# Deeper buffers in the second graph attention, and a two-part, one-step-later block ending in both attentions

## The chip, the cores and the metric

The kernel runs on one core of one Trainium2 chip. The metric is the device time of one launch in microseconds (us). A step of the work is written for five engines: TensorE (PE), VectorE (DVE), ScalarE (ACT), GpSimd (POOL) and SyncE (SP, which here only issues DMAs). Each engine takes its instructions strictly in the order in which they were recorded, and semaphores order the engines against each other.

## What is computed

Four layers run one after the other on 6250 nodes with 256 features each. Two of them are graph attentions over edges that are sorted by their destination; the change is in these two alone. Cut to what matters:

```python
x = x + gat0(layernorm(x), src, dst)          # first attention: 206250 edges, 4 heads of 64
x = x + routed_ffn(layernorm(x))              # 8 experts, top 2
x = x + weighted_sum(layernorm(x), src, dst, edge_weight)
x = x + gated_ffn(layernorm(x), edge_index)   # its gate is the second attention:
                                              # 131072 edges on 8192 node numbers, 4 heads of 4
# an attention, for every edge (s -> d) and head:
e     = leaky_relu(a_src[s] + a_dst[d])
p     = exp(e - segment_max(e, d)[d])
out_d = sum_over_edges(p * h[s]) / (sum_over_edges(p) + 1e-16)
```

In the last layer the 16 numbers of each node that come out of the second attention go through a layer norm, a mean over heads and a top 2 of 4, and the resulting gates weigh four dense expert outputs that were computed before.

## The kernel before, in words

**Tiles, pieces, blocks.** The sorted edges are cut into tiles of 128 edges, and Q = 8 tiles make a piece. The first attention has 1612 tiles (pieces 0 to 201), the second 787 (pieces 0 to 98, the last with 3 tiles). The nodes are cut into 49 blocks of 128 (0 to 48). For each tile, POOL gathers the rows of the 128 source nodes out of a table in device memory with one indirect DMA (`gathers`, L1299 to L1305).

**The loop.** `gat_stream` (from L1225) runs both attentions. It is a software pipeline written out by hand under `manual_schedule`: the order of instructions on each engine is the order of the Python calls. In step s_ it issues, in this order: the gathers of piece s_; on SP, every fourth step, the load of a batch of edge destinations (`load`, tiles db and kf); `beside()`, which hands in one item of other work; the functions that an earlier step left for this one (list `later`, L1463); for the first attention, `done` for blocks whose sums are whole (`ready`, L1466); `scores` of piece s_ - 2 (L1330 to L1343, DVE: it reads the gathered rows); `turned_hots` of piece s_ + 1 (tile ot); the first part of `sums` for piece q = s_ - 10 (PE: a matmul of each tile's one-hot matrix by its messages); `node_parts` of piece s_; `move_sums` (first attention only); `one_hots` of piece q + 1 (tile oh, L1184); the second part of `sums`; every fourth step the transposes and the two scans that find the greatest score, and `weights` (ACT's Exp, L1374 and L1378, and a DVE product, L1379); at the end of the step the block endings of the second attention, and `messages` of piece q + 1 (L1386 to L1393, DVE). So a piece's messages are made 9 steps, and its sums 10 steps, after its gathers were issued.

**Ending a block.** In the second attention the sums of a block lie in PSUM (tile acc, two buffers). When a block's last tile has been summed, its number goes into `ended`, and `done` (L1836) is called at the end of that step: DVE adds the three parts of the sums (tile a24, L1838), ACT takes an Exp (po, L1840), and DVE divides and combines (L1842 to L1855). On the last block of a group of four, `group` follows at once: the layer norm, the top 2 and the gates (`route`, from L767, 33 small DVE instructions with two turns through ACT), and four `put`s of four DVE instructions each (L1872) are left for `beside()`, with a DMA of the results after the fourth (L1882). `done` also issues on SP the load of that block's dense results, tile yb (L1831).

In the first attention windows of 16 tiles (two pieces) are summed, copied to SBUF by ACT (tile kept, L1422), and moved into the sums of the blocks that they touch by further matmuls (`move_sums`, tile bacc, two PSUM buffers, L1435). When a block is whole, `done` (L1969) runs at the start of the next step: ACT's Exp (po, L1972), seven DVE instructions (L1974 to L1985), the store of the block, and a spread (L1992 to L1996). `normed` (L2001 to L2002 and another spread), `twice` (PE transposes, ACT copy xT, L2012 to L2014) and `logits` follow in the next three steps. After block 43, and after the last, the selection of experts (`chosen`) goes on in later steps, a few DVE instructions a step (L268 to L309).

**Other work in the steps.** `beside()` of the first attention prepares expert parameters; that of the second finishes the dense experts (until about 5478 us) and then does the `put`s.

**Buffers.** A tile name in a pool has a fixed number of buffers, and an instruction that writes a buffer again waits for the last reader of what lay in it. Before the change the second attention has 14 buffers for gathered rows (g; the first has 13), 6 for turned one-hots (ot), 4 for one-hots (oh) and 3 for split messages (s3).

Of the kernel before, what the change touches and what calls it, by code (L numbers as in the profile page):

```python
# [20 lines left out]
F32 = mybir.dt.float32  # L21
BF = mybir.dt.bfloat16
I32 = mybir.dt.int32
I16 = mybir.dt.int16
AF = mybir.ActivationFunctionType
# [7 lines left out]
P = 128  # L33
# [38 lines left out]
def tile_kernel(ctx, tc, src_ins, out):  # L72
    nc = tc.nc
    x_in = src_ins["x"]
    N, D = x_in.shape
# [633 lines left out]
    H0, C0 = I["L0_gnn_att_src"].shape  # L709
    H1, C1 = I["L1_ffn_att_src"].shape  # L710
    D1 = H1 * C1
# [280 lines left out]
    Q = 8  # L992
# [230 lines left out]
    def gat_stream(s, H, CD, si, il, dl, tab, NI, early, done, parts=1, beside=None, pe=None):  # L1223
# [8 lines left out]
        W = DH + 2 * H  # L1232
# [6 lines left out]
        with ExitStack() as st:  # L1239
# [4 lines left out]
            nbw, sums_of, ready, moved = {}, {}, [], []  # L1244
# [10 lines left out]
            mp = pool("gw", 2)  # L1255
# [42 lines left out]

            def gathers(q):  # L1299
                t0, n = span(q)  # L1300
                g = piece[q] = mp.tile([P, Q, W], F32, name="g", bufs=13 if parts == 1 else 14)
                for j in range(n):
                    nc.gpsimd.indirect_dma_start(  # L1303
                        out=g[:, j, :DH + H], out_offset=None, in_=tab,
                        in_offset=bass.IndirectOffsetOnAxis(ap=si[:, t0 + j:t0 + j + 1], axis=0))  # L1305

            def turned_hots(q):
                t0, n = span(q)
                db = dbs.pop(q)
                turned[q] = []  # L1310
                for b, a, m in s.windows(t0, n):
                    o = mp.tile([P, Q * P], BF, name="ot", bufs=4 if s.group else 6)
                    nc.vector.tensor_scalar(o[:, :m * P], db[:, (a - t0) * P:(a - t0 + m) * P], nid[:, b:b + 1], None,  # L1313
                                            op0=OP.is_equal)
                    turned[q].append((b, a, m, o))
# [66 lines left out]
            def messages(q):  # L1382
                t0, n = span(q)
                i, o = divmod(t0, B)
                gh = piece[q][:, :n, :DH].rearrange("p n (h c) -> p n h c", h=H)
                nc.vector.tensor_mul(gh, gh, ps[0][:, o:o + n, :, None].to_broadcast([P, n, H, CD]))  # L1386
                g = piece.pop(q)
                if parts > 1:
                    s3 = split[q] = mp.tile([P, Q, parts, W], BF, name="s3", bufs=3)
                    for k in range(parts):  # L1390
                        nc.vector.tensor_copy(s3[:, :n, k], g[:, :n])  # L1391
                        if k + 1 < parts:
                            nc.vector.tensor_sub(g[:, :n], g[:, :n], s3[:, :n, k])  # L1393
                else:
                    split[q] = g
# [45 lines left out]
            with tc.manual_schedule():  # L1441
                if s.group:
                    load_nodes()
                load(0)
                for q in range(min(3, npiece)):
                    turned_hots(q)
                for q in range(min(2, npiece)):
                    node_parts(q)
                zts, dMs, pzs = {}, {}, {}
                last, s_, later = max(npiece + LAG, PB * nbatch + 7) + 1, -1, []  # L1450

                def follow(a):
                    if a is not None:
                        later.append(a)

                while s_ < last or later or moved or ready:
                    s_ += 1
                    if s_ < npiece:
                        gathers(s_)
                    if PB <= s_ + 3 < npiece:  # L1460
                        load(s_ + 3)
                    beside()
                    now, later[:] = list(later), []  # L1463
                    for f, a in now:
                        follow(f(*a))
                    while ready:  # L1466
                        b = ready.pop(0)
                        follow(done(b, sums_of.pop(b), items.pop(b), mp))
                    k, q = s_ - 2, s_ - LAG
                    if 0 <= k < npiece:  # L1470
                        scores(k)
                    i = k // PB - 1
                    at = k % PB if 0 <= i < nbatch else None
                    if 3 <= k + 3 < npiece and k >= 0:
                        turned_hots(k + 3)
                    beside()
                    if 0 <= q < npiece:
                        sums(q, 0)
                    if at == 2:
                        pzs[i] = turn_back(*dMs.pop(i))  # L1480
                    if 0 <= k and k + 2 < npiece:
                        node_parts(k + 2)
                    move_sums()
                    if at == 1:
                        dMs[i] = greatest(i, zts.pop(i))
                    if 0 <= q + 1 < npiece:
                        hots[q + 1] = one_hots(s, q + 1, mp, ips, dl, 3 if s.group else 4, F32 if parts == 1 else BF)
                    beside()
                    if 0 <= q < npiece:
                        sums(q, 1)  # L1490
                    if at == 0:
                        zts[i] = turn_scores(i)
                    if at == 3:
                        weights(i, pzs.pop(i))
                    beside()
                    if s.group:
                        keep_sums()
                    while ended:
                        b = ended.pop(0)
                        follow(done(b, acc.pop(b), items.pop(b), mp))  # L1500
                    if 0 <= q + 1 < npiece:
                        messages(q + 1)
                    beside()
                while beside():
                    pass
# [298 lines left out]
    def layer1_fast(s1, si, dl1, il1, HN, tab_1, y_d, rest):  # L1804
# [4 lines left out]
        with tc.tile_pool(name="g1f", bufs=1) as g1, tc.tile_pool(name="f1w", bufs=2) as fp:  # L1809
# [18 lines left out]
            def load_y(b):  # L1828
                if b < NT:
                    ys[b] = fp.tile([P, E1 + 1, D], F32, name="yb", bufs=GB + 1)  # L1830
                    nc.sync.dma_start(ys[b], y_d[b])  # L1831
# [2 lines left out]
                return HN[:, b, :D1]  # L1834

            def done(b, acc, hs_, mp):  # L1836
                a = mp.tile([P, D1 + 2 * H1], F32, name="a24")
                nc.vector.tensor_reduce(a, acc.rearrange("p s w -> p w s"), AX.X, OP.add)  # L1838
                po = mp.tile([P, H1], F32, name="po")
                nc.scalar.activation(po, a[:, W1:], AF.Exp, scale=-1.0)  # L1840
                rd = mp.tile([P, H1], F32, name="rd")
                nc.vector.scalar_tensor_tensor(rd, a[:, D1:W1], 1e-16, po, op0=OP.add, op1=OP.add)  # L1842
                nc.vector.reciprocal(rd, rd)

                def hd(x):
                    return x.rearrange("p (h c) -> p h c", h=H1)

                load_y(b)
                g = b // GB
                if g not in ag:  # L1850
                    ag[g] = fp.tile([P, GB, D1], F32, name="ag")
                o = mp.tile([P, D1], F32, name="o")
                nc.vector.tensor_mul(hd(o), hd(hs_), po[:, :, None].to_broadcast([P, H1, C1]))
                nc.vector.tensor_add(o, o, a[:, :D1])
                nc.vector.tensor_mul(hd(ag[g][:, b % GB, :]), hd(o), rd[:, :, None].to_broadcast([P, H1, C1]))  # L1855
                if b == blocks_in(g)[-1]:
                    group(g)
# [37 lines left out]
    def fast(flag_s0, last_d, dl_d):  # L1895
# [12 lines left out]
        with tc.tile_pool(name="gat0f", bufs=1) as g0:  # L1908
# [58 lines left out]
                return hs  # L1967

            def done(b, acc, hx, mp):  # L1969
                acc, hs, x = acc[:, 0], hx[:, 0], hx[:, 1]  # L1970
                po = mp.tile([P, H0], F32, name="po")
                nc.scalar.activation(po, acc[:, D + H0:], AF.Exp, scale=-1.0)  # L1972
                rd = mp.tile([P, H0], F32, name="rd")
                nc.vector.scalar_tensor_tensor(rd, acc[:, D:D + H0], 1e-16, po, op0=OP.add, op1=OP.add)  # L1974
                nc.vector.reciprocal(rd, rd)
                o = mp.tile([P, D], F32, name="o")

                def hd(a):
                    return a.rearrange("p (h c) -> p h c", h=H0)

                nc.vector.tensor_mul(hd(o), hd(hs), po[:, :, None].to_broadcast([P, H0, C0]))
                nc.vector.tensor_add(o, o, acc[:, :D])
                nc.vector.tensor_mul(hd(o), hd(o), rd[:, :, None].to_broadcast([P, H0, C0]))
                nc.vector.tensor_add(o, o, bias)
                nc.vector.scalar_tensor_tensor(x, o, 0.0, x, op0=OP.max, op1=OP.add)  # L1985
                nc.sync.dma_start(x_d[b * P:(b + 1) * P], x)
                return normed, (b, mp, x) + spread(mp, x)
# [319 lines left out]
```

## Time and profile before

| | us |
|---|---|
| median of the 7 runs shown (6468.51 to 6478.05) | 6474.33 |
| the profiled execution: its time / its span | 6476.74 / 6474.9 |
| first attention, POOL's gathers (first to last start) | 189.7 to 2233.9 |
| second attention, POOL's gathers (first to last start) | 5385.6 to 6390.8 |
| second attention, DVE busy from 5700 to 6300 | 458.9 of 600 |

The profile comes from one execution. A group's row gives the line, the engine, the operation, its output and inputs, how many there were, their busy time and mean duration in ns, and the idle time of the engine just before them with what ended that idle time ("issue": nothing that the profile shows). A timeline's row gives the start, the duration and the same names; a square bracket at its end holds the idle time before it and what ended it. Rows with xN are several like instructions, merged.

### The profile page before, as it was taken

The page shows a single profiled execution, that of the slowest core. Times are in us where ns is not written, and L with a number is a line of the kernel's source. Part 1 is how long each engine was busy: PE and PEld are TensorE (multiplying, and loading weights), DVE is VectorE, ACT ScalarE, POOL GpSimd, SP SyncE. Part 2 cuts the span into 40 slices and gives each one's busy share as a digit, 9 for nine tenths or more (in the row PEclk, how much of TensorE's full clock was granted, in tenths as well). Part 3 has the DMA queues.
Part 4 walks back from the last instruction along what each step waited for, and adds up shares of the span by engine and source line. Part 5 has one row for each costly group of instructions (what it writes and reads, how often), then busy time and mean ns, then how long its engine had stood idle before and what let it go on. Part 6 is the DMA issues. An engine that isn't in the chain of part 4 may idle for free.

```text
span 6474.9 us, 61956 instructions
## 1 busy us (share of the span) xinstructions
PE 3812.3 (59%) x17583; PEld 2863.5 (44%) x17583; DVE 4331.8 (67%) x10445; ACT 1204.3 (19%) x2770; POOL 4094.1 (63%) x4304
## 2 busy tenths in 40 slices
PE   4256666665666679999513777776777677111111
PEld 3144444444444558888402444444444445111111
DVE  5266666666666683444368888888888872777777
ACT  2011111112221112323100222222222222000000
POOL 0677777777777612232147777777777765777773
PEclk9677777778777789999756888887888888555555
DMA  4644445444444335557563444444444442222221
GB/s 131 143 146 144 147 146 148 146 147 146 147 146 144 110 105 196 185 185 235 186 205 113 128 126 129 128 129 125 128 128 127 127 118 84 54 76 76 76 76 56
DMA packets 495995, 856.25 MB, mean 132 GB/s; under 512 B 140310, under 2 KB 345303, under 8 KB 486134
## 3 DMA queue, kind: packets, MB, share of 16 engines
q0 software_dynamic: 190112, 461.21, 26.0%
q1 hardware_dynamic: 280226, 366.94, 17.1%
q10 hardware_dynamic: 25300, 24.00, 1.1%
q8 instruction: 143, 2.34, 0.1%
q14 instruction: 214, 1.75, 0.1%
HBM read 758.44 MB, written 95.50 MB: 132 GB/s over the span
## 4 chain that ended last, share of the span: by engine, by line
POOL 34%; DVE 18%; issue 17%; PE 15%; DMA 14%; ACT 1%; DVEq 0%; SPq 0%; ACTq 0%; POOLq 0%; another core or an unknown queue 0%
POOL g L234 17%; POOL g L1303 17%; DMA g<-tab,si 7%; PE py L647 5%; PE ph L634 4%; DVE g L1386 3%; DMA g<-tab_ef,si 2%; DVE run L2102 2%; PE acc L1409 2%; DMA g<-tab_1f,si1s 2%; DVE oh L1184 2%; DMA xc<-x_d 1%; DVE ot L1313 1%; PE pf L1772 1%; PE pf L1784 1%
## 5 line engine op out<-in xcount | busy, mean ns | idle before, releaser
L234 POOL DMA_INDIRECT g<-tab_ef,si x1616 | 1531.4, 948 | 620.9 <-issue 599.9
L1303 POOL DMA_INDIRECT g<-tab,si x1612 | 1554.3, 964 | 504.3 <-issue 414.3
L2102 DVE SCALAR_TENSOR_TENSOR run<-g,wab,run 128x256 f32<-128x256 f32 x2626 | 1264.2, 488 | 330.5 <-DMA g<-tab_ef,si 252.7
L1409 PE MATMUL acc<-g,oh 128*128 128x264 f32 x3224 | 1000.6, 464 | 307.9 <-DVE g L1386 238.8
L1409 PEld LDWEIGHTS acc<-g,oh 128*128 128x128 f32 x3224 | 719.2, 232 | 484.0 <-DVE g L1386 265.7
L1303 POOL DMA_INDIRECT g<-tab_1f,si1s x787 | 766.7, 974 | 250.1 <-issue 212.4
L2219 PE MATMUL acc<-run,oh 128*128 128x256 f32 x808 | 304.1, 514 | 690.9 <-DVE oh L2106 533.0
L1335 DVE TENSOR_TENSOR z<-g,nd 128x32 f32<-128x32 f32 (+1 forms) x301 | 58.0, 193 | 830.6 <-DMA g<-tab,si 687.3
L1409 PE MATMUL acc<-s,oh 128*128 128x72 bf16 x1267 | 106.4, 249 | 751.9 <-DVE s L1391 751.9
L2219 PEld LDWEIGHTS acc<-run,oh 128*128 128x128 f32 x808 | 191.4, 252 | 794.7 <-issue 462.9
L1772 PE MATMUL pf<-xt,w 128*128 128x512 f32 (+1 forms) x832 | 411.4, 628 | 101.0 <-ACT h L1777 100.9
L1386 DVE TENSOR_TENSOR g<-g,mix 128x2048 f32<-128x2048 f32 x202 | 458.9, 2272 | 0.0
L1409 PEld LDWEIGHTS <-oh 128*128 128x128 bf16 x1267 | 85.8, 127 | 763.7 <-issue 481.0
L1784 PE MATMUL pf<-w,h 128*128 128x256 f32 x1568 | 402.2, 401 | 0.0
L634 PE MATMUL ph<-xe,w 128*128 128x256 f32 x1664 | 377.0, 383 | 3.8 <-DVE xe L622 3.8
L647 PE MATMUL py<-w,h 128*128 128x256 f32 x1664 | 370.1, 380 | 0.0
L610 POOL DMA_INDIRECT xg<-tab_x,gi x104 | 118.3, 1137 | 350.2 <-PE pt L619 276.7
L634 PEld LDWEIGHTS ph<-xe,w 128*128 128x128 f32 x1664 | 317.5, 193 | 46.4 <-DVE xe L622 4.6
L1784 PEld LDWEIGHTS pf<-w,h 128*128 128x128 f32 x1568 | 289.3, 194 | 99.4 <-issue 67.1
L647 PEld LDWEIGHTS py<-w,h 128*128 128x128 f32 x1664 | 313.1, 191 | 39.4
L650 POOL DMA_INDIRECT tab_y<-y,so x104 | 111.9, 1076 | 268.4 <-DVE y L649 263.9
L1772 PEld LDWEIGHTS pf<-xt,w 128*128 128x128 f32 x832 | 164.4, 211 | 250.3 <-issue 124.4
(510 smaller groups left out, 6092.1 us busy)
## 6 DMA issues: line engine op xcount, KB each, us to landing
w<-in_L_ffn_W SPq DMA_DIRECT2D x104, 1024.0 KB
db<-s_d SPq DMA_DIRECT2D x74, 1024.0 KB
yb<-y_d SPq DMA_DIRECT2D x49, 640.0 KB
g<-tab_ef,si POOLq DMA_INDIRECT x1616
g<-tab,si POOLq DMA_INDIRECT x1612
y_d<-y SPq DMA_DIRECT2D x196, 128.0 KB
g<-tab_1f,si1s POOLq DMA_INDIRECT x787
yy<-tab_y SPq DMA_DIRECT2D x7, 1792.0 KB
```

Of the source, the lines that this page charges most:

```text
L234: nc.gpsimd.indirect_dma_start(out=dst, out_offset=None, in_=table, in_offset=bass.IndirectOffsetOnAxis(ap=si[:, t:t + 1], axis=0))
L610: nc.gpsimd.indirect_dma_start(out=xg[:, i, :], out_offset=None, in_=tab_x, in_offset=bass.IndirectOffsetOnAxis(ap=gi[:, 2 * j + i:2 * j + ...
L634: nc.tensor.matmul(ph, w1[:, k, f * P:(f + 1) * P], xe[:, k, :], start=(k == 0), stop=(k == KD - 1))
L647: nc.tensor.matmul(py, hs[f][:, i * P:(i + 1) * P], w2[:, f, :], start=(f == 0), stop=(f == FC - 1))
L1184: nc.vector.tensor_tensor(o[:, :m], ips[:, None, k * P:(k + 1) * P].to_broadcast([P, m, P]), dl[:, a:a + m, None].to_broadcast([P, m, P]), ...
L1303: nc.gpsimd.indirect_dma_start(out=g[:, j, :DH + H], out_offset=None, in_=tab, in_offset=bass.IndirectOffsetOnAxis(ap=si[:, t0 + j:t0 + j ...
L1386: nc.vector.tensor_mul(gh, gh, ps[0][:, o:o + n, :, None].to_broadcast([P, n, H, CD]))
L1409: nc.tensor.matmul(acc[b].rearrange("p s w -> p (s w)"), oh[:, t - a], m_, start=(t == lo), stop=(t == hi))
L1772: nc.tensor.matmul(ph[:, :n], w1[:, e, k, f * P:(f + 1) * P], xts[g][:, k, :n], start=(k == 0), stop=(k == KD - 1))
L1784: nc.tensor.matmul(py[:, :D], hs[g, e, f][:, j * P:(j + 1) * P], w2[:, e, f, :], start=False, stop=(f == FC - 1))
L2102: nc.vector.scalar_tensor_tensor(at[:, i] if j < Q - 1 else r[i], g[:, j, :], w, at[:, i], op0=OP.mult, op1=OP.add)
L2219: nc.tensor.matmul(acc[i], oh[:, k], r[k], start=(q % 2 == 0 and k == 0), stop=(last and k == 1))
```

## The change

The second attention gets 20 buffers for g, 9 for ot, 8 for oh and 4 for s3; those of the first attention stay. The block endings of the second attention are called at the start of the step after the one in which the block ended, in place of the end of that same step. In both attentions `done` is cut in two: it issues the Exp (in the second attention also the addition of the three parts and the load of yb), and returns a function `ending`, which the loop calls a step later and which holds the rest. In the second attention a24 and po get 4 buffers.

```diff
-                g = piece[q] = mp.tile([P, Q, W], F32, name="g", bufs=13 if parts == 1 else 14)
+                g = piece[q] = mp.tile([P, Q, W], F32, name="g", bufs=13 if parts == 1 else 20)
...
-                    o = mp.tile([P, Q * P], BF, name="ot", bufs=4 if s.group else 6)
+                    o = mp.tile([P, Q * P], BF, name="ot", bufs=4 if s.group else 9)
...
-                    s3 = split[q] = mp.tile([P, Q, parts, W], BF, name="s3", bufs=3)
+                    s3 = split[q] = mp.tile([P, Q, parts, W], BF, name="s3", bufs=4)
...
-                while s_ < last or later or moved or ready:
+                while s_ < last or later or moved or ready or ended:
...
                     while ready:
                         b = ready.pop(0)
                         follow(done(b, sums_of.pop(b), items.pop(b), mp))
+                    while ended:
+                        b = ended.pop(0)
+                        follow(done(b, acc.pop(b), items.pop(b), mp))
...
-                        hots[q + 1] = one_hots(s, q + 1, mp, ips, dl, 3 if s.group else 4, F32 if parts == 1 else BF)
+                        hots[q + 1] = one_hots(s, q + 1, mp, ips, dl, 3 if s.group else 8, F32 if parts == 1 else BF)
...
                     if s.group:
                         keep_sums()
-                    while ended:
-                        b = ended.pop(0)
-                        follow(done(b, acc.pop(b), items.pop(b), mp))
                     if 0 <= q + 1 < npiece:
                         messages(q + 1)
...
@@ in layer1_fast, the second attention @@
             def done(b, acc, hs_, mp):
-                a = mp.tile([P, D1 + 2 * H1], F32, name="a24")
+                a = mp.tile([P, D1 + 2 * H1], F32, name="a24", bufs=4)
                 nc.vector.tensor_reduce(a, acc.rearrange("p s w -> p w s"), AX.X, OP.add)
-                po = mp.tile([P, H1], F32, name="po")
+                po = mp.tile([P, H1], F32, name="po", bufs=4)
                 nc.scalar.activation(po, a[:, W1:], AF.Exp, scale=-1.0)
+                load_y(b)
+                return ending, (b, a, po, hs_, mp)
+
+            def ending(b, a, po, hs_, mp):
                 rd = mp.tile([P, H1], F32, name="rd")
...
-                load_y(b)
                 g = b // GB
...
@@ in fast, the first attention @@
             def done(b, acc, hx, mp):
-                acc, hs, x = acc[:, 0], hx[:, 0], hx[:, 1]
                 po = mp.tile([P, H0], F32, name="po")
-                nc.scalar.activation(po, acc[:, D + H0:], AF.Exp, scale=-1.0)
+                nc.scalar.activation(po, acc[:, 0, D + H0:], AF.Exp, scale=-1.0)
+                return ending, (b, acc[:, 0], hx[:, 0], hx[:, 1], po, mp)
+
+            def ending(b, acc, hs, x, po, mp):
                 rd = mp.tile([P, H0], F32, name="rd")
```

## The prediction

> **What bounds the kernel now.** I read the page's costliest groups first, then POOL's waits in each attention, then the timelines of the two tails, since everything that the change touches lies in the two attentions. The groups give POOL's part:
>
> ```profile
> L1303 POOL DMA_INDIRECT g<-tab,si x1612 | 1554.3, 964 | 504.3 <-issue 414.3
> L1303 POOL DMA_INDIRECT g<-tab_1f,si1s x787 | 766.7, 974 | 250.1 <-issue 212.4
> ```
>
> Busy and idle time of the second row together are 1016.8 us; without the 10.6 us ahead of the first gather that is 1006.2 us, and first to last gather starts span 5385.6 to 6390.8. So POOL does nothing but gathers there, each 0.974 us and about 0.305 us of gap. Are those gaps waits? POOL's waits between 5386 and 6392 us (line, releaser, total, times, longest):
>
> ```profile
> POOL g L1303 <- issue: 212.4, 697, 0.3
> POOL g L1303 <- DMA vec<-in_L_ffn_ln_gamma: 10.6, 1, 10.6
> POOL g L1303 <- DMA g<-tab_1f,si1s: 9.4, 31, 0.3
> POOL g L1303 <- DVE ot L1313: 7.9, 26, 0.3
> ```
>
> No wait but the first is longer than 0.3 us, the gap that a gather has with no releaser at all. A gather has never waited for a free buffer. The first attention shows the same (13.4 us ahead of its first gather, no other above 0.3), and its DVE waits 687.3 us for gathered rows at L1335. **In both attentions POOL's own pace is the bound, and what the other engines do shows only after the last gather.** Those two tails are the DVE's. The second, in the DVE's timeline:
>
> ```profile
> 6375.87 0.35 DVE L1333 TENSOR_REDUCE nd<-pd 128x64 f32<-128x192 f32 x1
> 6379.99 0.19 DVE L1335 TENSOR_TENSOR z<-g,nd 128x32 f32<-128x32 f32 x1 [3.77 <-DMA g<-tab_1f,si1s]
> ...
> 6382.42 0.22 DVE L1838 TENSOR_REDUCE a<-acc 128x24 f32<-128x72 f32 x1
> 6382.97 0.16 DVE L1842 SCALAR_TENSOR_TENSOR rd<-a,po 128x4 f32<-128x4 f32 x1 [0.33 <-ACT po L1840]
> ...
> 6390.67 0.29 DVE L1386 TENSOR_TENSOR g<-g,pe 128x128 f32<-128x128 f32 x1
> ...
> 6396.84 0.19 DVE L1335 TENSOR_TENSOR z<-g,nd 128x32 f32<-128x32 f32 x1
> ```
>
> At 6379.99 the DVE waits for rows for the last time (piece 96, step 98). Then it ends block 43 and runs the gates of its group (6382.42 to 6390.67), and when it reaches the scores of piece 97 at 6396.84 the rows are there. From there it is dense to 6469.64, where the last output DMA issues.
>
> **The change, part by part.**
>
> *Buffers.* Nothing waits for g on POOL, and in the second attention the DVE's largest waits for anything but gathered rows are for ACT (18.8 us at L1379, 16.1 us at L1842). 0 us, by the rows above; the pace hides the rest. If a wait for a buffer sat in the gaps, it would be at most 0.305 - 0.300 us on 786 gathers, 4 us.
>
> *Moved instructions in the steady part.* In the second attention a block's a24, po and yb load pass messages and, on SP, sometimes the next db and kf loads; the ending is a step later; in the first attention seven DVE instructions and the chain behind them (normed, xT, logits, the tab_x store on SP) are a step later. SP already issues out, yb, db, kf and two more yb in one bunch (5750.35 to 5754) a batch ahead of their use, and a step is about 10 us, so nothing comes late. All this is hidden by POOL's pace: 0 us.
>
> *Tail of the second attention, a hole.* Block 43 ends in step 98. Now a24 runs at the start of step 99, ahead of the scores of piece 97, but the ending and the gates only at the start of step 100, behind them. So the DVE is through with step 98 at 6382.42 + 1.96 (messages, 6390.67 to 6392.63) = 6384.38, does a24 and nd (0.22 + 0.35) and waits for piece 97 from about 6384.96. The last gather of piece 96 starts at 6377.09 and its rows are used at 6379.99, 2.90 us later; the last gather of piece 97 starts at 6387.07, so its rows come at 6389.97. **The DVE stands for 5.0 us, in which it now does gates,** and that work has to be done afterwards. With the sooner landing that the chain of waits has for the gather of 5547.91, 2.28 us, the hole is 4.4; with the longest DMA that the chain of waits shows for gathered rows here, 6.05 us, it is 8.2; with none at all (the DVE busy with something else) it is 0.
>
> *Tail of the second attention, stalls that go.* The 0.33 us between a24 and rd goes for blocks 43 to 47 (5 x 0.33 = 1.65): a step lies between. For block 48 it stays, as nothing else is left. The 0.43 us in which a24 of block 48 waits for PE at 6459.94 goes: the gates of 44 to 47 now come after the last messages and cover that matmul. The yb load of block 48 is nearer to its use: 7.63 us from a24 (6459.94) to the first product (6467.57), less 0.48 us that SP takes; the DMA of it and of out is done at 6463, 4.5 us after issue, so it still fits. Sum of this tail: 5.0 - 1.65 - 0.43 = **+2.9 us.**
>
> *Tail of the first attention.* The last gather starts at 2233.89, the DVE's last wait for rows is 2.35 us at 2232.16. Shifted from before that wait to after it: the logits of block 44 and one step's share of the select (2228.06 to 2229.46), +1.4. Then ACT, where L1379 waits for it:
>
> ```profile
> 2253.70 0.37 ACT L2014 COPY xT<-mix 128x256 f32<-128x256 f32 x1 [5.17 <-PE mix L2012]
> 2254.09 1.28 ACT L1374 ACT_TABLE_LOAD   x1
> 2255.38 0.26 ACT L1374 ACTIVATE mix<-zt 128x128 f32<-128x128 f32 x1
> 2255.55 0.19 ACT L1378 ACTIVATE g<-zt 128x32 f32<-128x32 f32 x1
> ```
>
> The xT copy, queued ahead of the Exp in the same step, waits for a long row of matmuls; the DVE stands 2.30 us, and 0.94 us in the same place at 2282.46. A step later for xT parts the two. In its place normed's sd stands ahead of the Exp: sd 0.33, from the load to L1379 1.69 (2254.09 to 2255.78), less the one-hot (1.13) that the DVE does meanwhile, leaves 0.9 us each time. 2.30 + 0.94 - 1.8 = 1.4 gained. At the end, po of block 48 (2295.45) now stands behind both sd of block 47 and a table load; following the new order with the old durations I get 47's Exp at about 2289.1, its ending (3.2), sd, normed and sd (0.35 + 1.45 + 0.35), load 1.28, and po at 2296.0, +0.5. Sum: 1.4 - 1.4 + 0.5 = **+0.5 us**; from -3 (every such ACT stall gone, the shift hidden) to +4 (neither gain, the end 2 us worse).
>
> *Two rules of the Trainium skill.* The built order has 46 fewer ACT table loads, 1.28 us each in the rows with the Exp 0.01 us behind: 59 us of ACT time, hidden but for what is summed above. "ScalarE: Activation LUTs" (What ACT_TABLE_LOAD costs) puts a switch at about 2.66 us with a drain; by that it would be 122 us, just as hidden.
> Against the zero for moved DVE work: no gather took over 1.222 us (median 0.944) beside one-hots of 1.2 us. "SBUF — State Buffer" (SBUF: two separate sides) says that a DVE instruction in a two-port mode shuts GpSimd out of writing descriptors until it ends. By that (an estimate) moving 49 endings beside other gathers could shift the pace by up to 49 x 1.2 = 59 us either way, and the sum with it; the rows show no such lockout, so by them it stays 0.
>
> **Sum.** 2.9 + 0.5 = +3.4 us on the profiled execution (span 6474.9, time 6476.74) gives 6480.1. That execution lies 2.4 us above the median of the runs, so against the median it is 6474.33 + 3.4 = **6477.7, about 6478.**
>
> **Rivals.**
> 1. *The hole doesn't open* (rows land as early as 6385, or other work fills it). Then only stalls go: -2.1 + 0.5, 6473. For it: gathers of 3 tiles less crowd the queues at the end. Against: POOL issues piece 97's last gather only at 6387.07.
> 2. *The second attention is bound by the DVE*, so that its stalls count all along: 49 x 0.33 = 16.1 us gone, 6458. For it: the DVE is busy 459 of 600 us from 5700 to 6300. Against: it waits 122.4 + 14.3 us for rows or issue at L1335.
> 3. *The buffers speed POOL up*: gathers at the shortest 0.940 in place of 0.974 us would save 787 x 0.034 = 27 us, 6448. Nothing in the rows ties the excess to buffers.
> 4. *Slower: PSUM in the first attention.* A bacc buffer is now read by an ending at the start of the very step whose `move_sums` wants it for the block after next. PE waits for rd, its reciprocal and two products (2236.96 to 2238.09, 1.13 us) once a block. This is dear only once PE's sums come so late that gathers wait for one of 13 buffers. They are freed at step s - 3, some 30 us of slack. If all 47 counted: 53 us, 6527; half of them, 6501.
>
> **Chances.** Forecast (6474 to 6484) 0.54; rival 1 0.28; rival 2 0.05; rival 3 0.03; rival 4 or POOL's pace slower by 10 ns a gather (2399 x 0.010 = 24 us, 6498) 0.10. Holes of 4.4 to 8.2 and a first tail of -3 to +4 give -0.7 to +10.1, so 6473.6 to 6484.4 for the likeliest case; with the spread of the runs shown (about 6 down, 4 up) and rival 1 the range is 6466 to 6490. About 0.2% (13 us) is what a measurement of this kernel can tell from no change: faster takes rivals 2 and 3, slower takes rival 4: 0.08, 0.82, 0.10.
>
> **What would show it.** Right: gathers of both attentions from first to last start as long as before (1005.2 and 2044.2 us); a DVE wait of about 5 us at L1335 near the end of the second attention with the gates behind it; rd no longer waiting for po but once; the wait of L1379 at the first tail under 1 us. Wrong: any POOL wait over 0.3 us at L1303, or a mean spacing other than 1.269 and 1.279 us.

## The result, and the profile after

The changed kernel takes 6490.07 us (median of 14 runs, 6485.34 to 6497.56), the kernel before 6473.84 us beside it (34 runs). The ratio is 1.0026, 95% interval 1.0019 to 1.0033: slower by some 16 us, where 3.4 were forecast. In some of the runs below every kernel, the one before included, takes 7.6 to 7.8 ms with a lower granted TensorE clock beside it ("low-clock runs"), and these say nothing of a difference of 10 us.

The two gather rows of the page after:

```profile
L1303 POOL DMA_INDIRECT g<-tab,si x1612 | 1562.2, 969 | 504.0 <-issue 422.2
L1303 POOL DMA_INDIRECT g<-tab_1f,si1s x787 | 769.5, 978 | 250.2 <-issue 213.6
```

Number and idle time are as before; the busy time grew by 7.9 and 2.8 us. The gathers became longer, not more often late. POOL's waits in the first attention (line, releaser, total, times, longest) show the same:

```profile
POOL g L1303 <- issue: 421.9, 1385, 0.3
POOL g L1303 <- DVE Z L1339: 32.6, 107, 0.3
POOL g L1303 <- DMA s_nb<-NB: 13.3, 1, 13.3
```

Nothing but the first gather waits over 0.3 us, so no buffer was short. Where the time lies, in the profiled executions of both kernels and of four experiments told below (us; from first to last starts of the gathers):

| | before | after | first att. alone | second alone | before + copy | after + copy |
|---|---|---|---|---|---|---|
| ahead of the first gather | 189.7 | 190.4 | 192.5 | 190.8 | 191.7 | 192.1 |
| first attention's gathers | 2044.2 | 2052.0 | 2055.7 | 2044.7 | 2028.0 | 2027.6 |
| its tail, to the next layer's first gather | 137.8 | 139.4 | 140.4 | 137.9 | 139.8 | 140.5 |
| layers between (code unchanged) | 3013.8 | 3015.9 | 3010.4 | 3009.3 | 3009.9 | 3014.6 |
| second attention's gathers | 1005.3 | 1008.1 | 1004.5 | 1007.5 | 996.6 | 994.2 |
| its tail | 84.0 | 86.4 | 84.7 | 86.3 | 85.9 | 86.8 |
| span | 6474.9 | 6492.1 | 6488.1 | 6476.5 | 6451.9 | 6455.9 |

After against before: gathers +7.8 and +2.8, tails +1.6 and +2.3. The unchanged layers between scatter by 6.6 us over the six columns, so a profile's span alone can't show 5 us. The stages scatter less. The first attention's gathers run the same code in columns 2 and 3 (3.7 us apart) and in columns 1 and 4 (0.5 us); the second's in columns 1 and 3 (0.8 us) and, but for the buffer counts, in 2 and 4 (0.6 us).

**What makes a gather longer.** The trace has each gather beside the DVE's instructions. Here are POOL and then the DVE of the changed kernel in the same 4 us:

```profile
864.48 0.96 POOL L1303 DMA_INDIRECT g<-tab,si  x1 [0.30 <-issue]
865.75 1.23 POOL L1303 DMA_INDIRECT g<-tab,si  x1 [0.30 <-DVE R L1355]
867.28 0.95 POOL L1303 DMA_INDIRECT g<-tab,si  x1 [0.30 <-issue]
```

```profile
864.15 0.48 DVE L1313 TENSOR_SCALAR ot<-db,s_nid 128x1024 bf16<-128x1024 int16 x1
864.54 0.95 DVE L1355 TENSOR_TENSOR_SCAN R<-kf,zt 128x384 f32<-128x384 bf16 x1
865.53 0.69 DVE L1358 TENSOR_TENSOR_SCAN M<-kf,R 128x256 f32<-128x256 bf16 x1
866.25 0.29 DVE L1361 TENSOR_TENSOR d<-zt,M 128x128 f32<-128x128 f32 x1
866.46 1.21 DVE L1184 TENSOR_TENSOR oh<-ips,dl 128x1024 f32<-128x1024 f32 x1
867.59 2.28 DVE L1386 TENSOR_TENSOR g<-g,mix 128x2048 f32<-128x2048 f32 x1
```

The gather of 865.75 starts under the second scan (M, from two SBUF inputs) and takes 1.23 us in place of 0.945. The next starts under the one-hots (0.39 us of them still to go), whose ips lies in PSUM, and takes 0.95. Over both traces, of gathers that start more than 0.11 us after an instruction's start and more than 0.25 us before its end: under M all are prolonged (44 of 44 before, 63 of 63 after), under ot all (50 of 50, 54 of 54), under the first scan R, which reads zt in PSUM, none (0 of 18, 0 of 11). Not every instruction that works in SBUF alone prolongs them: under bs (the statistics of 256 columns, one SBUF input, 0.43 us long) none of 49 is longer by more than 0.02 us. The excess over 0.945 us is what the instruction still has to run less 0.13 us (ot: on average 0.306 to go, 0.176 of excess) or less 0.19 us (M, after: 0.447 and 0.254).

| gathers above 0.955 us, and their summed excess | first attention | second |
|---|---|---|
| before | 246, 30.5 us | 211, 23.8 us |
| after | 321, 38.1 us | 215, 26.7 us |

The differences, +7.7 and +2.9 us, are the growth of the gathers. By the instruction that a gather's start meets, in the first attention: M 8.6 to 11.2 us (32 to 42 of its 49 runs), ot 8.7 to 12.9. So 6.8 of the 7.7 us lie in these two, which were not moved. The moved instructions, the ending's products and the layer norms (xt) behind them, prolong gathers too, by 12.1 us before and 13.2 after.

**Why the change moves them.** A step of the DVE begins when gathered rows land, so it is tied to POOL's cadence. The DVE's waits for rows in the first attention, before and then after:

```profile
DVE z L1335 <- DMA g<-tab,si: 687.3, 171, 8.7
```

```profile
DVE z L1335 <- DMA g<-tab,si: 715.6, 196, 8.8
```

With an ending of 3 us in one step, 171 of 202 steps began with a wait; with the ending cut and spread, 196. More steps are locked to POOL at the same distance, and at that distance ot and M lie across a gather's start. That the lock is the reason for the higher count is read from these rows and not tested by itself.

**Theories.** A (phase): the above; the moved instructions change which DVE instruction a gather's start meets. B: the buffers, or their new places in SBUF, cost the time. C: only the tails count. D: POOL's pace has nothing to do with when the DVE's instructions run.

### The profile page after: what moved, and what is told of

It reads as the page before. It is cut to its first block, busy times and chain, and to the rows that moved or that the text cites. A ratio compares the mean times of both kernels' runs of the same rounds, so it can differ in the third digit from the quotient of the medians.

```text
span 6492.1 us, 61929 instructions
## 1 busy us (share of the span) xinstructions
PE 3790.7 (58%) x17583; PEld 2841.3 (44%) x17583; DVE 4322.5 (67%) x10445; ACT 1142.7 (18%) x2724; POOL 4104.9 (63%) x4304
## 4 chain that ended last, share of the span: by engine, by line
POOL 38%; issue 19%; PE 14%; DVE 14%; DMA 14%; ACT 1%; DVEq 0%; POOLq 0%; SPq 0%; ACTq 0%; another core or an unknown queue 0%
POOL g L1303 21%; POOL g L234 17%; DMA g<-tab,si 6%; PE ph L634 5%; PE py L647 5%; DMA g<-tab_ef,si 3%; DVE run L2107 2%; DMA g<-tab_1f,si1s 2%; DVE g L1386 1%; DVE oh L1184 1%; PE acc L1409 1%; DMA xc<-x_d 1%; PE bacc L1435 1%; DMA tab_y<-y,so 1%; PE ph L1956 1%
## 5 line engine op out<-in xcount | busy, mean ns | idle before, releaser
L1409 PE MATMUL acc<-g,oh 128*128 128x264 f32 x3224 | 966.7, 452 | 382.3 <-DVE g L1386 196.2
L1409 PEld LDWEIGHTS acc<-g,oh 128*128 128x128 f32 x3224 | 704.3, 227 | 541.5 <-DVE g L1386 211.7
L2224 PEld LDWEIGHTS acc<-run,oh 128*128 128x128 f32 x808 | 192.5, 254 | 798.0 <-issue 466.1
L1409 PEld LDWEIGHTS <-oh 128*128 128x128 bf16 x1267 | 85.9, 127 | 677.6 <-issue 351.5
```

The lines of the kernel that those rows point to most:

```text
L1409: nc.tensor.matmul(acc[b].rearrange("p s w -> p (s w)"), oh[:, t - a], m_, start=(t == lo), stop=(t == hi))
L2224: nc.tensor.matmul(acc[i], oh[:, k], r[k], start=(q % 2 == 0 and k == 0), stop=(last and k == 1))
```

## The experiments

**1. The first attention's ending alone.** Before, with only this edit:

```diff
             def done(b, acc, hx, mp):
-                acc, hs, x = acc[:, 0], hx[:, 0], hx[:, 1]
                 po = mp.tile([P, H0], F32, name="po")
-                nc.scalar.activation(po, acc[:, D + H0:], AF.Exp, scale=-1.0)
+                nc.scalar.activation(po, acc[:, 0, D + H0:], AF.Exp, scale=-1.0)
+                return ending, (b, acc[:, 0], hx[:, 0], hx[:, 1], po, mp)
+
+            def ending(b, acc, hs, x, po, mp):
                 rd = mp.tile([P, H0], F32, name="rd")
```

> The kernel before with only the first attention's ending cut in two and called a step later, in a call of its own. Theory A (phase): first attention's gathers 2052 us in place of 2044 (+8) with some 321 gathers above 0.955 us, its tail +1.5, the second attention as before (1005.3), time +9 to +10. Theory B (buffers): within 2 us of before. Theory C (tails alone): +0.5 to +1.5.

Measured: 6490.06 us against 6476.81, ratio 1.0023 (1.0014 to 1.0032). The page's rows:

```profile
L1303 POOL DMA_INDIRECT g<-tab,si x1612 | 1565.9, 971 | 505.7 <-issue 421.0
L1303 POOL DMA_INDIRECT g<-tab_1f,si1s x787 | 765.9, 973 | 250.2 <-issue 212.4
```

The first attention's gathers are 11.5 us longer (342 above 0.955 us, excess 42.2 us), the second's are not. Its DVE waits for rows 195 times. This edit alone gives most of the loss; B and C can't, as there is no buffer in it and its two tails are +2.6 and +0.7. A's sign and place hold. The expected 8 us are 3.5 short, which is about the 3.7 us by which the two profiles of this code differ.

**2. The second attention's later ending alone**, without the four larger buffer counts:

```diff
-                while s_ < last or later or moved or ready:
+                while s_ < last or later or moved or ready or ended:
...
+                    while ended:
+                        b = ended.pop(0)
+                        follow(done(b, acc.pop(b), items.pop(b), mp))
...
@@ and done and ending of the second attention as in the change, a24 and po with 4 buffers @@
```

> The last try of the kernel before with only the second attention's ending called a step later and cut in two (a24 and po with 4 buffers), without the four larger buffer counts. On a chip on which the kernel before takes about 6475 us: Theory A (phase): first attention's gathers 2044 us within 1, the second's 1008 in place of 1005.3 (+2.8), the tail with its hole near 5 us +2.3, time +5. Theory B (buffers): gathers 1005.3, tail +2.3, so +2.3, the other 2.8 being the buffers'. On a chip on which it takes about 7650 us the run tells neither.

Measured: 6477.20 us, ratio 1.0001 (0.9992 to 1.0010), so -5 to +6 us: the time can't tell +5 from +2.3. The stages can: first attention's gathers 2044.7 (+0.5), the second's +2.2, tail +2.3. What hid it in the profile are the unchanged layers, 4.5 us shorter than in the profile of before. The whole change has +2.8 there, so 0.6 us is left for buffers, no more than the scatter: no cost of B's size. The two moves measured singly, ratios 1.0023 and 1.0001, also make up nearly the whole 1.0026.

**3. The buffers alone** (20 g, 9 ot, 8 oh, 4 s3), measured twice, both in low-clock runs:

> The kernel before with only the four larger buffer counts of the second attention (20 g, 9 ot, 8 oh, 4 s3), in a call of its own. Theory A (phase): no DVE instruction and no gather changes its place: within 2 us of before, gathers 2044 and 1005 within 1 us. Theory B (buffers or their places in SBUF cost the time): the 2.8 us of the second attention's gathers, or more, are here: +3 to +10 us.

Measured: 7653.37 us, ratio 1.0041 (1.0027 to 1.0055), and in the other measurement 1.0061 (1.0037 to 1.0084). In these runs the first attention's gathers stand for the first time ahead of the 105th, when 13 buffers of 8 tiles are full, and then for 3 to 4 us about once in 16. No gather does so in the profiles of the result. So here gathers do wait for buffers, which is not the case of the forecast. That the deeper buffers cost 0.4 to 0.6% in it is measured; the cause wasn't tried.

**4. A shift by a copy that nothing reads, first placing.** One DVE instruction is added to every step of the changed kernel, PSUM to PSUM, so that it prolongs no gather itself (ips is made wider for it):

```diff
                 nc.vector.scalar_tensor_tensor(z[:, :n], z[:, :n], 0.2, z[:, :n], op0=OP.mult, op1=OP.max)
+                m = 160 if parts == 1 else 80
+                nc.vector.tensor_copy(ips[:, 2 * P:2 * P + m], ips[:, :m])
                 i, o = divmod(t0, B)
```

> The changed kernel with one DVE instruction added in every step of both attentions, behind the second z instruction: a copy from PSUM to PSUM of 160 columns (second attention) or 80 columns (first) that nothing reads. It moves the later DVE instructions of a step by some 0.2 to 0.3 us against POOL's gathers. Theory A (phase: a gather that starts under certain DVE instructions is prolonged until they end): the trace of the changed kernel with those DVE instructions moved by 0.2 to 0.4 us gives a summed excess over 0.945 us of 1 to 13 us in place of 32 in the first attention, and 5 to 20 in place of 19 in the second. So the time falls by 15 to 35 us against the changed kernel (6490), to 6455 to 6475, although some 300 instructions were added; first attention's gathers 2020 to 2035 us in place of 2052. Theory D (when DVE instructions run is nothing to POOL's pace): gathers 2052 and 1008 us within 1 us, time 0 to +1 us against the changed kernel.

(The text has the two widths the wrong way round: 160 in the first attention, 80 in the second.) Measured: 6498.52 us, ratio to before 1.0031 (1.0021 to 1.0041), some 3 us above the changed kernel's 1.0026, where 15 to 35 us less were expected. The first attention's gathers went to 2061.9 us (excess 48.4 in place of 38.1), the second's to 1002.6 (21.2 in place of 26.7). D falls with that, since adding DVE work that POOL doesn't touch moved the pace by +9.9 and -5.4 us; but A's number failed as well. Its DVE rows say why:

```profile
1014.38 0.19 DVE L1336 SCALAR_TENSOR_TENSOR z<-z 128x32 f32<-128x32 f32 x1
1014.48 0.32 DVE L1338 COPY ips<-ips 128x160 f32<-128x160 f32 x1
1014.72 0.18 DVE L1341 TENSOR_TENSOR Z<-z,nd 128x32 f32<-128x32 f32 x1
1014.82 0.48 DVE L1313 TENSOR_SCALAR ot<-db,s_nid 128x1024 bf16<-128x1024 int16 x1
```

From z to ot it is 0.44 us, against 0.34 in the changed kernel (863.81 to 864.15): the copy lies in the stall between z and the Z that needs it, so the shift was 0.1 us and not 0.3. With 0.11 us the same working (all prolonging DVE instructions of the trace moved against the gathers) gives 32.4 to 41.0 us and 19.4 to 11.6 us of excess, the signs and nearly the sizes measured. That was worked out afterwards, so it needed a run of its own.

**5. The same, behind the stall, on the changed kernel.** The copy now follows Z, with 230 and 80 columns.

> Again the changed kernel with a PSUM-to-PSUM copy that nothing reads behind the Z instruction of every step, 230 columns in the first attention (a shift of about 0.3 us), 80 in the second (about 0.15 us), now in a call of its own, since in the calls of four kernels every kernel's gathers, those of the kernel before too, stood for some 4 us once in 16. Theory A (a gather that starts under certain DVE instructions is prolonged until they end, so the phase between DVE and POOL counts): modelled excess 32.4 to 1.3 us in the first attention, 19.4 to 4.0 in the second; so gathers from 2052 to about 2021 and from 1008 to about 992, the time 40 to 50 us below the changed kernel, 6440 to 6450. Theory D (no tie between DVE and POOL's pace): 0 to +1 us against the changed kernel, 6490.

Measured: 6456.51 us, ratio to before 0.9970 (0.9959 to 0.9981), about 34 us below the changed kernel. The DVE's rows and the page's:

```profile
1009.19 0.19 DVE L1336 SCALAR_TENSOR_TENSOR z<-z 128x32 f32<-128x32 f32 x1
1009.41 0.19 DVE L1339 TENSOR_TENSOR Z<-z,nd 128x32 f32<-128x32 f32 x1
1009.52 0.40 DVE L1341 COPY ips<-ips 128x230 f32<-128x230 f32 x1
1009.83 0.47 DVE L1313 TENSOR_SCALAR ot<-db,s_nid 128x1024 bf16<-128x1024 int16 x1
```

```profile
L1303 POOL DMA_INDIRECT g<-tab,si x1612 | 1537.7, 954 | 505.5 <-issue 432.4
L1303 POOL DMA_INDIRECT g<-tab_1f,si1s x787 | 755.7, 960 | 250.3 <-issue 217.0
```

From z to ot it is 0.64 us, a shift of 0.30. 301 added instructions, and POOL's gathers are some 24 and 14 us faster: excess 13.9 us (115 gathers) and 12.9 us (159). Of 15 gathers that start well under such a copy, in this run and the next, none is prolonged. A's mechanism holds. Its size was too large by some 10 us: the copy leaves collisions that the working didn't count.

**6. The same copy on the kernel before.**

> The kernel before with the PSUM-to-PSUM copy that nothing reads behind the Z instruction (230 columns in the first attention, 80 in the second), in a call of its own. Theory A (phase): as the changed kernel with the same copy went from 6490 to 6456.5 with its gathers' excess at 13.9 and 12.9 us, before goes from 30.5 and 23.8 to about 14 and 12 us: gathers 2028 and 993, and with its shorter tails (3.8 us together) the time is 6446 to 6454, so 3 to 10 us below the changed kernel with the copy: the changed order costs then only its tails. If the changed order has a cost of its own beside phase and tails, the difference is over 10 us. Theory D: 6474.

Measured: 6453.45 us, ratio 0.9964 (0.9952 to 0.9977), the fastest version found; gathers 2028.0 and 996.6. Against the kernel before they fell by 16.2 and 8.7 us, and their summed excess by 16.2 and 8.6 (to 14.2 and 15.2 us). With the copy in both, the changed order is 3 to 6 us slower (6456.51 against 6453.45; 20.0 and 26.2 us below their own runs of before, 6476.53 and 6479.66). The gathers are within 0.4 and 2.3 us of each other. So the changed order has no large cost beside phase and tails.

**7. Does the kind of operand decide?** The changed kernel, with the scans' intermediate R left in PSUM, so that the second scan has one SBUF input in place of two:

```diff
+                nc.scalar.copy(ips[:, 3 * P:], zt[:, 1])
                 return zt
...
-                R = mp.tile([P, 3 * P], F32, name="R")
-                nc.vector.tensor_tensor_scan(R, kf[:, :3 * P], zt.rearrange("p k e -> p (k e)"), 0.0,
+                R = zt.rearrange("p k e -> p (k e)")
+                nc.vector.tensor_tensor_scan(R, kf[:, :3 * P], R, 0.0,
...
-                nc.vector.tensor_sub(d, zt[:, 1], M[:, :P])
+                nc.vector.tensor_sub(d, ips[:, 3 * P:], M[:, :P])
```

> Once more the changed kernel with the intermediate R of the two scans left in PSUM, in hope of a chip on which the kernel before takes about 6475 and not 7650 us. Theory A, narrow (operand kinds decide which DVE instructions prolong a gather): the 42 and 21 collisions with the second scan, 11.2 and 4.8 us, go; time 10 to 16 us below the changed kernel, gathers about 2041 and 1003. Theory A, wide (any long DVE instruction that a gather's start meets prolongs it): within 3 us of the changed kernel. Theory D: 0 to +2.

All three measurements are low-clock runs (7778.95 us, ratio 1.0106, 1.0087 to 1.0124; the others 7773.57 and 7777.16, 1.0116 and 1.0132), so the time it saves stays open. The collisions can be counted all the same. POOL and then DVE of the first of them:

```profile
2124.85 0.95 POOL L1303 DMA_INDIRECT g<-tab,si  x1 [0.30 <-issue]
2126.10 0.95 POOL L1303 DMA_INDIRECT g<-tab,si  x1 [0.30 <-issue]
```

```profile
2124.92 0.96 DVE L1356 TENSOR_TENSOR_SCAN zt<-kf,zt 128x384 f32<-128x384 bf16 x1 [1.74 <-issue]
2125.92 0.69 DVE L1359 TENSOR_TENSOR_SCAN M<-kf,zt 128x256 f32<-128x256 bf16 x1
```

The gather of 2126.10 starts 0.18 us into M, with 0.51 us of M to go, and takes 0.95 us. Over the three traces 38 gathers start under this M (0.69 us long, as before) and none is prolonged; in a low-clock run of the changed kernel with the copy of experiment 5, 19 of 19 are under M from two SBUF inputs. Under ot, which wasn't edited, all are in all of them (13, 14 and 17). So for this scan the operand decides, not the instruction's length or the state of the run. "SBUF — State Buffer" of the Trainium skill (SBUF: two separate sides) says that a DVE instruction with two SBUF inputs contends with a GpSimd instruction that reads SBUF, but it infers that a tensor_tensor doesn't hold up the writing of descriptors, where here the tensor_tensor o<-o,bias, from SBUF alone, prolonged all 24 gathers that start well under it in the kernel before, and the measurement decides. The figures of how much a gather loses are these runs'.

**The other runs** are all low-clock runs, in which gathers wait for buffers; no theory is told apart by them. Ratios to before, with their intervals. The first attention's split, twice: 1.0015 (0.9994 to 1.0036) and 1.0013 (0.9994 to 1.0032).

> The kernel before with only the first attention's block ending cut in two (the ending one step later); second attention and buffers as before. Theory A (phase): a gather on POOL that starts while certain DVE instructions run is prolonged until that instruction ends, and the later ending changes which DVE instruction meets a gather's start. Then the first attention's gathers take as long as in the changed kernel, first to last start 2052 us in place of 2044.2 (+8), with 321 gathers or so above 0.955 us in place of 246; its tail +1.5; the second attention's gathers stay at 1005.3. Time about +9 us. Theory B (buffers and where they lie in SBUF cost the time): within 2 us of before. Theory C (only the tails count): +0.5 to +1.5 us, gathers 2044.

> Again the kernel before with only the first attention's ending cut in two, since in the first try the gathers of every kernel, the one before included, stood for 3 to 5 us once in some 16 and no difference of 10 us could be read. Theory A (phase): first attention's gathers 2052 us in place of 2044 (+8), its tail +1.5, the rest as before, time +9. Theory B (buffers): within 2 us of before. Theory C (tails): +0.5 to +1.5.

The second attention's later ending, three times: 1.0058 (1.0035 to 1.0081), 1.0040 (1.0023 to 1.0057), 1.0036 (1.0016 to 1.0055).

> The kernel before with only the second attention's block ending called a step later and cut in two (a24 and po with 4 buffers as in the change); first attention and the four larger buffer counts as before. Theory A (phase): first attention's gathers 2044 us, second attention's gathers 1008 in place of 1005.3 (+2.8), tail with the hole of some 5 us at L1335 near its end +2.3; time about +5 us. Theory B (buffers): gathers of the second attention 1005, only the tail's +2.3. Theory C (tails): the same +2.3.

> The kernel before with only the second attention's ending called a step later and cut in two (a24 and po with 4 buffers), the four larger buffer counts left out, in a call of its own. Theory A (phase): first attention's gathers as before (2044 us within 1), the second's 1008 in place of 1005.3 (+2.8), the tail with its hole near 5 us +2.3, time +5. Theory B (buffers): gathers 1005.3, tail +2.3, so +2.3, the other 2.8 being the buffers'. Theory C: +2.3.

> Once more the kernel before with only the second attention's ending called a step later and cut in two (a24 and po with 4 buffers), the four larger buffer counts left out; if the chip is one on which the kernel before takes about 6475 us: Theory A (phase): first attention's gathers 2044 us within 1, the second's 1008 in place of 1005.3 (+2.8), the tail with its hole near 5 us +2.3, time +5. Theory B (buffers): gathers 1005.3, tail +2.3, so +2.3, the other 2.8 being the buffers'.

The buffers alone, the other measurement: 1.0061, as above.

> The kernel before with only the four larger buffer counts of the second attention (20 g, 9 ot, 8 oh, 4 s3); no instruction is moved. Theory A (phase): no DVE instruction and no gather changes its place, 0 us, within 2 us of before, gathers 2044 and 1005. Theory B (buffers or their places in SBUF cost the time): +3 to +10 us, seen in the second attention's gathers. Theory C: 0 us.

The copy in its first place, on the kernel before (the widths are the wrong way round here too): 0.9958 (0.9936 to 0.9981).

> The kernel before with one DVE instruction added in every step of both attentions, behind the second z instruction: a copy from PSUM to PSUM of 160 columns (second attention) or 80 columns (first) that nothing reads. It pushes the later DVE instructions of the step back by some 0.2 to 0.3 us against the gathers. Theory A (phase): with all DVE instructions of the trace moved by 0.3 us, the summed excess of the first attention's gathers over 0.945 us falls from about 30 to below 15 us, and that of the second from 24 to between 5 and 20; so despite some 300 added instructions the time falls by 10 to 30 us, or at least the gathers' sum of busy time changes by over 5 us in either attention. Theory D (POOL's pace has nothing to do with when DVE instructions run): the gathers keep 2044 and 1005 us within 1 us, and the time is 0 to +1 us.

The copy behind the stall, on the kernel before 0.9993 (0.9975 to 1.0011), on the changed kernel 1.0141 (1.0113 to 1.0169).

> The kernel before with the PSUM-to-PSUM copy that nothing reads placed behind the Z instruction, where no stall of a dependent instruction swallows it, and wider: 230 columns in the first attention (a shift of about 0.3 us for all that follows in the step), 80 in the second (about 0.15 us). Theory A (phase): the trace of before, with the prolonging DVE instructions moved by these amounts, leaves 2.6 of 23.8 us of modelled excess in the first attention and 3.0 of 19.5 in the second. So gathers' excess above 0.945 us falls from 30.5 to about 9 and from 23.8 to about 7, the gathers from 2044 to about 2023 and from 1005 to about 989, the time by 30 to 40 us, to 6435 to 6450. Theory D (no tie between DVE and POOL's pace): 0 to +1 us. If the prolonging comes from any DVE instruction at all and not from the kinds named: no clear fall.

> The changed kernel with the same copy behind the Z instruction, 230 columns in the first attention and 80 in the second. Theory A (phase): modelled excess 32.4 to 1.3 us in the first attention, 19.4 to 4.0 in the second; so gathers from 2052 to about 2021 and from 1008 to about 992, the time 40 to 50 us below the changed kernel, 6440 to 6450, and within 10 us of the kernel before with the same shift: the changed order is then no slower but for its tails (+2 to +4). Theory D: 0 to +1 us against the changed kernel.

The second scan with an input from PSUM, the two other measurements: 1.0116 (1.0092 to 1.0140), 1.0132 (1.0107 to 1.0156).

> The changed kernel with the intermediate R of the two scans left in PSUM (the first scan writes over its input; ACT copies the middle third of it aside before): the second scan, which took two SBUF inputs, now has one from PSUM like the first scan. No DVE instruction moves by more than the changed durations. Theory A in its narrow form (only DVE instructions of certain operand kinds prolong a gather; two SBUF inputs do, a PSUM input does not): the 42 and 21 collisions with the second scan, 11.2 and 4.8 us, go; time 10 to 16 us below the changed kernel, 6474 to 6480, gathers 2041 and 1003. Theory A in its wide form (any long DVE instruction that a gather's start meets prolongs it): no change within 3 us. Theory D: +0 to +2.

> The changed kernel with the intermediate R of the two scans left in PSUM (the first scan writes over its input; ACT copies its middle third aside before), in a call of its own: the second scan then has one input from PSUM, like the first, in place of two from SBUF. Theory A, narrow (operand kinds decide which DVE instructions prolong a gather): the 42 and 21 collisions with the second scan, 11.2 and 4.8 us, go; time 10 to 16 us below the changed kernel, 6474 to 6480, gathers about 2041 and 1003. Theory A, wide (any long DVE instruction that a gather's start meets prolongs it): within 3 us of the changed kernel. Theory D: 0 to +2.

## Why the prediction was wrong

**The step that failed** is the second rule: "the rows show no such lockout, so by them it stays 0". The rows did show it. I tested the lockout on one-hots of 1.2 us, which read PSUM and prolong nothing, and passed over the instructions from SBUF alone; the very spread quoted there (0.944 median, 1.222 longest; 1.226 in the first attention) was the lockout, 30.5 and 23.8 us of it already in the kernel before. From it followed the 0 us for moved instructions in the steady part. In its place: +7.8 and +2.8 us. The page's rule was the better guide, though the 59 us worked out by it were far too many, since only gathers that start under such an instruction lose, and only the rest of it.

**What bounds the kernel** was right: POOL's pace in both attentions, no wait over 0.3 us. That is why 5 ns a gather make 8 us. The sign by which the text wanted to be shown wrong has come: 1.274 and 1.283 us from gather to gather in place of 1.269 and 1.279.

**Buffers, 0 us:** right as far as the stages show (0.6 us left for them); measured alone only in low-clock runs.

**Tail of the second attention, +2.9 us:** measured +2.3, and +2.3 with the later ending alone. The hole, in the DVE's timeline after:

```profile
6400.56 0.23 DVE L1838 TENSOR_REDUCE a<-acc 128x24 f32<-128x72 f32 x1
6400.70 0.35 DVE L1333 TENSOR_REDUCE nd<-pd 128x64 f32<-128x192 f32 x1
6404.71 0.19 DVE L1335 TENSOR_TENSOR z<-g,nd 128x32 f32<-128x32 f32 x1 [3.66 <-DMA g<-tab_1f,si1s]
...
6410.92 0.15 DVE L1846 SCALAR_TENSOR_TENSOR rd<-a,po 128x4 f32<-128x4 f32 x1
6411.11 0.18 DVE L1847 RECIPROCAL rd<-rd 128x4 f32<-128x4 f32 x1
```

a24 and nd ahead of the wait, the ending and the gates behind it, as forecast; the hole is 3.66 us, not 5.0. rd waits for po once (0.3 us). That the sum comes within 0.6 us although the hole was 1.3 us smaller is partly luck: the stalls saved 1.8 us and not 2.1 (rd waited 1.7 us before, a24 0.4), and some 0.5 us stays unexplained.

**Tail of the first attention, +0.5 us:** measured +1.6, in its range. The DVE's waits in it:

```profile
2263.04 0.19 DVE L1379 TENSOR_TENSOR g<-zt,il 128x32 f32<-128x32 f32 x1 [0.93 <-ACT g L1378]
2290.43 0.19 DVE L1379 TENSOR_TENSOR g<-zt,il 128x32 f32<-128x32 f32 x1 [0.93 <-ACT g L1378]
2298.90 0.16 DVE L1979 SCALAR_TENSOR_TENSOR rd<-bacc,po 128x4 f32<-128x4 f32 x1 [1.80 <-ACT po L1974]
2305.66 0.16 DVE L1979 SCALAR_TENSOR_TENSOR rd<-bacc,po 128x4 f32<-128x4 f32 x1 [1.85 <-ACT po L1974]
```

The 2.30 us at L1379 fell to 0.93 as worked out. New are two waits for po, 1.8 us each: with nothing left to lie between, a later ending waits for ACT.

**Rivals.** 1 didn't come (the hole opened), nor 2. 3 asked the right question, what makes gathers longer than their shortest, and had no answer. 4 gave the right place, POOL's pace, under "PSUM", at 10 ns a gather; it was 4.9 and 3.6 ns. Its mechanism is out: no gather waited, and only two of PE's weight loads for bacc (L1435) waited for an ending's read of it (o, L1987), 0.50 and 0.52 us, both after the last gather. The range ended at 6490 for want of this term.

## What to carry to other kernels

Where POOL issues indirect gathers without a pause, DVE instructions whose operands all lie in SBUF can lengthen the gather that starts under them, by the rest of their own run less 0.13 to 0.19 us. Here those with two SBUF inputs did, and the tensor_scalar ot; the statistics bs didn't. Count the gathers above the usual duration and name the DVE instruction under each start, before you call moved DVE work hidden. In a loop that is locked to POOL's cadence a shift of 0.1 to 0.3 us of a whole step is worth as much as the change itself (here +10 to -24 us in one attention). One operand in PSUM took the second scan out of the matter; what that saves in time wasn't measured.

## What the runs showed of the hardware

- An added DVE instruction a step, PSUM to PSUM and read by nobody, made the kernel 0.36% faster (0.23 to 0.48%), by the phase: the fall of the gathers' time is that of their excess (experiment 6).
- An independent DVE instruction between two dependent ones cost 0.1 us where it took 0.32: it fills the stall of the second.
- It goes both ways: a gather under way can prolong the DVE's instruction. In the kernel before, ot of 128x1024 takes 0.48 us (median of 299); 19 took over 0.50 us, all of them beside a gather, the longest 0.70 us with a gather that had begun 0.50 us before it.
